# Eight segments instead of seven, nineteen sorted groups instead of sixteen, and two PSUM areas for the late read-back, in a graph-convolution kernel

## The chip, the cores and the metric

One NeuronCore of a Trainium2 chip runs the whole program; no other core takes part. Times are device microseconds of one execution. The kernel before has a median of 4145.89 us over 3 runs (4143.61 to 4146.77). The engines are named as in the profile: PE (TensorE matmul), PEld (its weight load), DVE (VectorE), ACT (ScalarE), POOL (GpSimd), SP (SyncE, which here only issues DMAs).

## What is computed

A continuous-filter convolution over 12500 nodes with 128 features and 412500 directed edges. The edges are sorted by `dst`; `src` is random. The aggregation is by `src`, and the gather by `dst`:

```python
h   = relu(layernorm(x)) @ W_in2f                      # 12500 x 128
Wij = (ssp(edge_attr @ W_f1 + b_f1) @ W_f2 + b_f2) * edge_weight[:, None]
agg = segment_sum(h[dst] * Wij, src, 12500)            # the random side
out = x + ssp(agg @ W_o1 + b_o1) @ W_o2 + b_o2         # ssp = softplus - log 2
```

So the gather reads neighbouring rows, while the sum goes to random nodes.

## The kernel before

**Chunks and groups.** Edges are taken in chunks of 512 (`CH`), four chunks to a group, 203 groups, 810 chunks with edges in them. One loop step `k` does one chunk's message and looks ahead for the later ones: hidden layer and its logarithm (PE, ACT), window matrix `at` (DVE), block matrix `inb` (DVE), rank `free`/`top` (PE, DVE), gather product `picked` (PE, ACT), `product` (DVE), transposes `turned` (PE), scaling into `o` (DVE, L925) and at last the scatter.

**Scatter.** Each message row goes to a slot in a table in HBM that belongs to the node's block of 128 nodes. For a plain chunk `message` issues four indirect DMAs from POOL, one for each 128 rows (L938). `o` has four buffers of two chunks each, and the small copy of the place column into `o` (L932) is the first write into a buffer, so it is there that DVE waits if POOL has not yet sent the chunk that was in the buffer before.

**Sorted groups.** The groups in `SORTED` (16 before) are first permuted by matmuls so that the rows of one block come together; they hold 4 x 480 edges in place of 4 x 512. Half of each such chunk goes out with one static DMA from SP, and only two indirect DMAs a chunk remain on POOL (L1067). The permuting (classes `Permute`, `Permuted`) is spread over the 18 steps ahead of the group, on DVE and PE.

**Segments and read-back.** The groups are cut into segments (`SEGS`), each with a table of its own. A table holds `T` tiles of 128 rows for each of the 98 node blocks (one more for the blocks near the segment's own nodes); `T` follows from the messages that the segment may send to a block. Nine steps after a segment's last chunk its table begins to be read back: for each unit of one to four tiles an SP load (`load`, L1317), a DVE comparison of the place column with the node numbers (`compare`, L1339), and for each tile one fp32 matmul that sums the rows into a PSUM area, three blocks side by side (`add`, L1357). The end of such three blocks is called an *end* here: DVE then adds the area to the sums in SBUF (`keep`, L1380). Only one area is there, `room_ps`, the part of the bank `count_ps` that the constant does not use, and the unit after an end goes into the next step, after that `keep`.

**What sets the read-back's pace.** A small planner at the end of the function spreads the tiles of all segments but the last over the steps, as evenly as the segment ends allow; a step takes at most three units and, before, at most one end. From its lines the numbers are

| segment: groups, sorted | T | units, tiles | tiles a step in its stretch |
|---|---|---|---|
| 55, 8 | 10 | 294, 1012 | 6.33 from step 229 |
| 37, 4 | 7 | 196, 710 | 6.33 to step 500 |
| 31, 4 | 6 | 260, 868 | 7.12 from step 501 |
| 29, 0 | 6 | 196, 612 | 7.12 to step 708 |
| 23, 0 | 5 | 196, 506 | 7.63 from step 709 |
| 14, 0 | 3 | 98, 310 | 7.63 to step 816 |
| 14, 0 | 3 | 98, 304 | read after the loop |

**After the loop.** The last segment is read with nothing beside it, four blocks (one *quad*) to a bank, banks taken in turn from the tags `acc` and `v`. For each quad `finish` runs the output layers in five stages, one stage of five different quads per turn (`stages`): `z_out` (PE, L555) with three ACT passes, `r_out` (DVE, L560), `v_out` (PE, L564), the addition to x (DVE, L568), the store.

Of the kernel before, what the change touches and what calls it, by code (L numbers as in the profile page):

```python
# [10 lines left out]
F32 = mybir.dt.float32  # L11
# [7 lines left out]
P = 128  # L19
# [1 line left out]
CH = 512  # L21
NCHUNK = TG * P // CH
QT = CH // P
SEGS = (55,37,31,29,23,14,14)
RW = P + 1
VIEWS = 16
BG = 8
# [10 lines left out]
HQ = 9  # L38
PV = 120
WIN = PV * QT  # L40
SORTED = (*range(6,51,6),*range(63,91,7),*range(97,122,7))
NPG = len(SORTED)
FIXED = 2 * P
NEAR = 2 * P
# [22 lines left out]
def gnn_kernel(  # L67
# [588 lines left out]
    with tc.tile_pool(name="edge", bufs=2) as edge, tc.tile_pool(  # L656
        name="quad", bufs=3
# [629 lines left out]
        class Collect:  # L1287


            def __init__(self, seg):  # L1290
                self.seg = seg
                self.size = QT if seg is segs[-1] else QT - 1

                self.units = []
                b = 0
                while b < NBLK:
                    T = seg.read(b)
                    n = next(n for n in (4, 3, 2, 1)
                             if n == 1 or n * T <= UT and b % self.size % n == 0
                             and b % self.size + n <= self.size  # L1300
                             and b + n <= NBLK and seg.read(b + n - 1) == T)
                    k = ceil_div(T, UT)
                    cuts = [T * i // k for i in range(k + 1)]
                    self.units += [(b, n, t0, t1 - t0) for t0, t1 in zip(cuts, cuts[1:])]
                    b += n
                self.m, self.to, self.acc, self.done = {}, {}, {}, []
                self.banks = [("acc", 1)]
# [36 lines left out]
            def add(self, u):  # L1344
                b0, nb, t0, nt = self.units[u]
                m, to = self.m.pop(u), self.to.pop(u)
                for j in range(nb * nt):
                    b, t = b0 + j // nt, t0 + j % nt
                    i = b % self.size
                    if i == 0 and t == 0 and self.size < QT:  # L1350
                        self.acc[b // self.size] = room_ps
                    elif i == 0 and t == 0:
                        tag, bufs = self.banks[b // QT % len(self.banks)]
                        self.acc[b // QT] = psum.tile([P, QT, P], F32, name="acc", tag=tag,
# [35 lines left out]

        summed = []
        owed = []

        made = {}

# [136 lines left out]
        todo = []  # L1532
# [8 lines left out]
        units[k] = [todo[0][1:]]  # L1541
        while i < len(todo):
            k += 1
            while i < len(todo) and todo[i][0] < k and len(units.get(k, ())) < 3:
                if i + 1 < len(todo):
                    units.setdefault(k, []).append(todo[i + 1][1:])
                else:
                    units.setdefault(k, [])
                i += 1
                if todo[i - 1][1].ends(todo[i - 1][2]):  # L1550
                    break

        def x_ahead(homes):
# [276 lines left out]
```

## Time and profile before

| | us |
|---|---|
| median of 3 runs | 4145.89 |
| the profiled execution, its own time | 4140.92 |
| its span, first to last instruction | 4139.20 |
| POOL busy | 3008.6 (73%), 3132 instructions |
| PE busy | 3535.6 (85%) |
| DVE busy | 3452.6 (83%) |
| ACT busy | 1549.9 (37%) |
| DMA | 845.03 MB, mean 204 GB/s |

The span is 1.7 us below the execution's own time, and that is 5.0 us below the median of the runs shown. In the page a busy PE is modelled, and POOL's busy time leaves out what its own sequencer does between two instructions; so shares of the whole span do not say alone which engine sets the pace. For that the rows must be read by stages, with what each engine waits for.

### The profile page before, as it was taken

Reading aid. Unit: us, or ns where it says so; the run is one execution under the profiler, and the core shown is the slowest. Engines: PE = TensorE matmul, PEld = TensorE weight load, DVE = VectorE, ACT = ScalarE, POOL = GpSimd, SP = SyncE. Lnnn points to the kernel's source line nnn. Section 1 sums busy time; section 2 is a strip of 40 time slices with the busy share of each in tenths; the row PEclk is TensorE's granted clock in tenths of the full one; section 3 lists DMA queues with packets and bytes.
Section 4 is the critical chain, followed back from the end, with each engine's and each line's share of the span. In section 5 each row is a group of like instructions: output and inputs, shape, how many; then the busy total and the mean of one; then the engine's idle time right before and its main releaser. Section 6 shows DMA issues by size and latency. Waiting matters only on the chain. (4 is left out here: it accounts for less than half of the span.)

```text
span 4139.2 us, 66733 instructions
## 1 busy us (share of the span) xinstructions
PE 3535.6 (85%) x18966; PEld 2206.5 (53%) x18966; DVE 3452.6 (83%) x8858; ACT 1549.9 (37%) x2365; POOL 3008.6 (73%) x3132
## 2 busy tenths in 40 slices
PE   5777777777789999988998999898998889888978
PEld 2333333333355666655565665565665556565667
DVE  7988988887689888888999988787888878888866
ACT  3444444444334334433333333333333323333313
POOL 4777777777777777777777777777777777777740
PEclk8888989888899999999999999999999999999989
DMA  6787565666577778877778776667766867666666
GB/s 162 209 267 231 157 171 160 181 196 197 161 195 217 220 228 258 242 206 201 204 240 254 215 210 183 174 181 242 202 196 203 256 204 217 194 182 193 182 188 189
DMA packets 628969, 845.03 MB, mean 204 GB/s; under 512 B 218036, under 2 KB 461868, under 8 KB 628592
## 3 DMA queue, kind: packets, MB, share of 16 engines
q1 hardware_dynamic: 528431, 634.82, 55.6%
q0 software_dynamic: 99584, 205.74, 14.8%
q8 instruction: 153, 2.51, 0.3%
q14 instruction: 225, 1.84, 0.2%
q10 hardware_dynamic: 576, 0.13, 0.0%
HBM read 426.42 MB, written 413.84 MB: 203 GB/s over the span
## 5 line engine op out<-in xcount | busy, mean ns | idle before, releaser
L938 POOL DMA_INDIRECT slots<-o,slot x2984 | 2882.1, 966 | 949.2 <-issue 707.5
L1357 PEld LDWEIGHTS count_ps<-to,m 128*128 128x128 f32 (+1 forms) x8036 | 1004.4, 199 | 660.5 <-DVE to L1339 418.0
L1357 PE MATMUL count_ps<-to,m 128*128 128x128 f32 (+1 forms) x8036 | 1114.8, 291 | 214.8 <-DVE to L1339 171.9
L907 ACT ACTIVATE hg<-picked 128x512 f32<-128x512 f32 x810 | 481.0, 594 | 2032.6 <-PE picked L901 1882.6
L895 PE MATMUL v<-r,wf 128*128 128x512 f32 x1620 | 891.9, 634 | 6.6 <-ACT r L804 4.0
L1339 DVE TENSOR_TENSOR to<-count_ps,m 128x384 f32<-128x384 f32 (+5 forms) x1396 | 716.5, 557 | 19.4 <-PE count_ps L1357 11.5
L913 DVE SCALAR_TENSOR_TENSOR product<-v,bf_t,hg 128x512 f32<-128x512 f32 x810 | 600.7, 742 | 100.4 <-PE v L895 80.8
L920 PE MATMUL turned<-ident,product 128*128 128x128 f32 x3240 | 521.9, 286 | 26.6 <-ACT hg L907 26.2
L809 DVE TENSOR_TENSOR inb<-count_ps,blk 128x392 f16<-128x392 f32 x746 | 414.4, 556 | 131.1 <-PE count_ps L1357 91.7
L925 DVE TENSOR_TENSOR o<-turned,rcut 128x512 f32<-128x512 f32 x746 | 506.4, 679 | 0.9 <-PE turned L920 0.9
L920 PEld LDWEIGHTS turned<-ident,product 128*128 128x128 f32 x3240 | 396.5, 147 | 204.8 <-issue 117.1
L804 ACT ACTIVATE r<-r,half 128x1024 f32<-128x1024 f32 x405 | 465.3, 1149 | 13.2
L803 ACT ACTIVATE r<-z,bf 128x1024 f32<-128x1024 f32 x405 | 448.7, 1108 | 0.0
L795 PE MATMUL z<-f,wf 20*128 20x512 f32 x1492 | 432.2, 655 | 0.0
L840 DVE TENSOR_REDUCE top<-free 128x4 f32<-128x392 f32 x746 | 412.6, 553 | 3.5 <-PE free L835 3.5
L901 PE MATMUL picked<-at,near 96*128 96x512 bf16 x746 | 298.5, 400 | 100.3 <-DVE o L925 82.2
L868 PE MATMUL free<-inb,rest_of 128*128 128x392 f16 x778 | 268.5, 345 | 114.1 <-DVE top L840 109.6
L895 PEld LDWEIGHTS v<-r,wf 128*128 128x128 f32 x1620 | 301.6, 200 | 109.1 <-issue 22.5
L795 PEld LDWEIGHTS z<-f,wf 20*128 20x128 f32 x1492 | 114.7, 187 | 295.8 <-issue 291.0
L887 DVE TENSOR_SCALAR at<-rel,prow 96x512 bf16<-96x512 bf16 x746 | 267.0, 358 | 0.0
L835 PE MATMUL free<-inb,after 128*128 128x392 f16 x746 | 257.7, 345 | 6.6 <-DVE used L874 4.6
L932 DVE COPY o<-place 128x8 f32<-128x8 f32 x373 | 72.3, 194 | 212.8 <-DMA slots<-o,slot 207.0
(226 smaller groups left out, 2235.9 us busy)
## 6 DMA issues: line engine op xcount, KB each, us to landing
m<-slots SPq DMA_DIRECT2D x822, 193.5 KB
m<-slots SPq DMA_DIRECT2D x336, 258.0 KB
rel<-rel_d SPq DMA_DIRECT2D x187, 384.0 KB
slots<-zero SPq DMA_DIRECT2D x100, 516.0 KB
slots<-o,slot POOLq DMA_INDIRECT x2984
f<-in_f_n SPq DMA_DIRECT2D x404, 80.0 KB
slots<-zero SPq DMA_DIRECT2D x158, 193.5 KB
slots<-zero SPq DMA_DIRECT2D x74, 258.0 KB
```

The costliest lines, as they stand in the source:

```text
L795: nc.tensor.matmul(z[:, k, :], wf1[rows, :], self.f[rows, :], start=True, stop=True)
L803: nc.scalar.activation(r, z, AF.Exp, bias=bf1, accum_out=exps[:, i:i + 1])
L804: nc.scalar.activation(r, r, AF.Ln, bias=half, scale=0.5)
L809: nc.vector.tensor_tensor(inb, count_ps[:, None, :NBLK].to_broadcast([P, QT, NBLK]), self.blk[:, c * QT:(c + 1) * QT, None].to_broadcast([ ...
L895: nc.tensor.matmul(v, wf2, r, start=True, stop=True)
L907: nc.scalar.activation(hg, ps, AF.Copy)
L913: nc.vector.scalar_tensor_tensor(m, v, bf2_t, hg, op0=ALU.add, op1=ALU.mult)
L920: nc.tensor.transpose(ps[:, i, :], m[:, i * P:(i + 1) * P], ident)
L925: nc.vector.tensor_mul(o[:, :, :P], ps, rcut.to_broadcast([P, QT, P]))
L938: put = nc.gpsimd.indirect_dma_start(out=views[j % VIEWS], out_offset=bass.IndirectOffsetOnAxis(ap=self.slot[:, j:j + 1], axis=0), in_=o[: ...
L1339: nc.vector.tensor_tensor(to[:p, a:e, :], count_ps[:p, None, :].to_broadcast([p, e - a, P]), self.m[u][:p, a:e, P:].to_broadcast([p, e - a ...
L1357: nc.tensor.matmul(self.acc[b // self.size][:, i, :], m[:p, j, :P], to[:p, j, :], start=t == 0, stop=t == self.seg.read(b) - 1)
```

## The change

Three things change.

1. `SEGS` becomes (56,36,38,29,14,14,8,8), and `SORTED` 19 groups: 6 to 54 by sixes and 62 to 125 by sevens. The sum stays 203 groups; since three more groups hold 480-edge chunks there are 811 chunks with edges. 76 chunks are sorted and 735 plain, against 64 and 746.
2. For a segment whose first group lies two or more past the last sorted group (the flag `twin`, here the segments of 29, 14, 14, 8 and 8 groups), the areas of the read-back alternate: every second one is a bank of the tag `acc`, which the sorting and the first part of the program use earlier.
3. In the planner a step may then take two ends in place of one; three units stay the limit.

```diff
-SEGS = (55,37,31,29,23,14,14)
+SEGS = (56,36,38,29,14,14,8,8)
...
-SORTED = (*range(6,51,6),*range(63,91,7),*range(97,122,7))
+SORTED = (6, 12, 18, 24, 30, 36, 42, 48, 54, 62, 69, 76, 83, 90, 97, 104, 111, 118, 125)
...
             def __init__(self, seg):
                 self.seg = seg
                 self.size = QT if seg is segs[-1] else QT - 1
+                self.twin = seg.g0 > permuted[-1] + 1
...
                 for j in range(nb * nt):
                     b, t = b0 + j // nt, t0 + j % nt
                     i = b % self.size
+                    if i == 0 and t == 0:
+                        turns.append(b)
                     if i == 0 and t == 0 and self.size < QT:
-                        self.acc[b // self.size] = room_ps
+                        if self.twin and len(turns) % 2:
+                            self.acc[b // self.size] = psum.tile([P, QT, P], F32, name="acc")
+                        else:
+                            self.acc[b // self.size] = room_ps
...
+        turns = []
...
             k += 1
+            ends = 0
             while i < len(todo) and todo[i][0] < k and len(units.get(k, ())) < 3:
...
                 i += 1
-                if todo[i - 1][1].ends(todo[i - 1][2]):
+                ends += todo[i - 1][1].ends(todo[i - 1][2])
+                if ends > todo[i - 1][1].twin:
                     break
```

The same planner with the new numbers gives:

| segment: groups, sorted | T | units, tiles | tiles a step in its stretch |
|---|---|---|---|
| 56, 9 | 10 | 294, 1012 | 5.82 from step 233 |
| 36, 5 | 7 | 196, 710 | 5.82 to step 528 |
| 38, 5 | 7 | 294, 966 | 8.28 from step 529 |
| 29, 0 | 6 | 196, 612 | 8.28 |
| 14, 0 | 3 | 98, 310 | 8.28 to step 756 |
| 14, 0 | 3 | 98, 310 | 8.57 from step 757 |
| 8, 0 | 2 | 68, 204 | 8.57 to step 817 |
| 8, 0 | 2 | 54, 206 | read after the loop |

In all 4330 tiles in 1298 units, against 4322 in 1338. The table of zeros that clears the tables ahead of their use grows from 630 to 648 DMAs.

**POOL's queue, from the third segment's last sorted groups to the end.** `slots_123` is the table of the third segment, `slots_124` and on those of the later ones; a row stands for as many indirect DMAs as its last number says. Before:

```order
L1067 DMA slots_123<-o,slot_p 82432x129 x8
L938 DMA slots_123<-o,slot 82432x129 x64
L938 DMA slots_124<-o,slot 78336x129 x464
L938 DMA slots_125<-o,slot 64768x129 x368
L938 DMA slots_126<-o,slot 39680x129 x224
L938 DMA slots_127<-o,slot 38912x129 x216
```

and now:

```order
L1067 DMA slots_123<-o,slot_p 96000x129 x8
L938 DMA slots_123<-o,slot 96000x129 x64
L938 DMA slots_124<-o,slot 78336x129 x464
L938 DMA slots_125<-o,slot 39680x129 x224
L938 DMA slots_126<-o,slot 39680x129 x224
L938 DMA slots_127<-o,slot 26112x129 x128
L938 DMA slots_128<-o,slot 26368x129 x124
```

Over the whole queue 2984 plain and 128 sorted indirect DMAs became 2940 and 152, so 3112 became 3092.

**DVE in a late step of the loop, while a table is read.** `to` is the result of a comparison, `agg` the sums, `count_ps` the old area (`room_ps` is in its bank) and `acc` the new one. Before, in the reading of the sixth segment (units of 3 tiles, one end to a step):

```order
L913 SCALAR_TENSOR_TENSOR product<-v,bf_t,hg 128x512
L840 TENSOR_REDUCE top<-free 128x4
L1380 TENSOR_TENSOR agg<-agg,count_ps 128x384
L887 TENSOR_SCALAR at<-rel,prow 96x512
L809 TENSOR_TENSOR inb<-count_ps,blk 128x392
L1339 TENSOR_TENSOR to<-count_ps,m 128x384 x3
L925 TENSOR_TENSOR o<-turned,rcut 128x4x128
```

and now, in the reading of the seventh (units of 4 and 2 tiles):

```order
L913 SCALAR_TENSOR_TENSOR product<-v,bf_t,hg 128x512
L840 TENSOR_REDUCE top<-free 128x4
L1386 TENSOR_TENSOR agg<-agg,acc 128x384
L1386 TENSOR_TENSOR agg<-agg,count_ps 128x384
L887 TENSOR_SCALAR at<-rel,prow 96x512
L809 TENSOR_TENSOR inb<-count_ps,blk 128x392
L1340 TENSOR_TENSOR to<-count_ps,m 128x256
L1340 TENSOR_TENSOR to<-count_ps,m 128x512
L1340 TENSOR_TENSOR to<-count_ps,m 128x256
L925 TENSOR_TENSOR o<-turned,rcut 128x4x128
```

A step with two ends has two additions to `agg`, one from each area; the rest of the step stands as it did.

**PE in the reading after the loop, one quad** (numbers kept: `to_...` tells which comparison a sum waits for). Before:

```order
L555 MATMUL z_out_49136<-agg_13464,wo1_64 128x512
L564 MATMUL v_out_49723<-wo2_65,r_out_49632 128x128 x4
L1357 MATMUL acc_49712<-to_49703,m_49665 128x128 x3
L1357 MATMUL acc_49712<-to_49710,m_49687 128x128 x3
L1357 MATMUL acc_49712<-to_49732,m_49694 128x128 x3
L1357 MATMUL acc_49755<-to_49739,m_49701 128x128 x3
```

and now:

```order
L555 MATMUL z_out_49938<-agg_13814,wo1_64 128x512
L564 MATMUL v_out_50358<-wo2_65,r_out_50291 128x128 x4
L1363 MATMUL acc_50346<-to_50336,m_50280 128x128 x4
L1363 MATMUL acc_50377<-to_50344,m_50303 128x128 x4
```

On DVE, with which these sums are paired, the rows before are

```order
L560 SCALAR_TENSOR_TENSOR r_out_49675<-z_out_49136,nbo1_71,r_out_49675 128x512
L568 TENSOR_TENSOR xo_29964<-xo_29964,v_out_49680 128x512
L1339 TENSOR_TENSOR to_49732<-count_ps_157,m_49694 128x384
L1339 TENSOR_TENSOR to_49739<-count_ps_157,m_49701 128x384
L1339 TENSOR_TENSOR to_49746<-count_ps_157,m_49708 128x384
```

and now

```order
L568 TENSOR_TENSOR xo_31505<-xo_31505,v_out_50296 128x512
L1340 TENSOR_TENSOR to_50336<-count_ps_156,m_50280 128x512
L1340 TENSOR_TENSOR to_50344<-count_ps_156,m_50303 128x512
L1386 TENSOR_TENSOR agg_13814<-agg_13814,acc_50315 128x512
L560 SCALAR_TENSOR_TENSOR r_out_50322<-z_out_49938,nbo1_71,r_out_50322 128x512
L568 TENSOR_TENSOR xo_31625<-xo_31625,v_out_50327 128x512
```

A quad of the plain blocks has two units of 4 tiles in place of four of 3. Before, two of its four comparisons (`to_49732`, `to_49739`) stand behind the same turn's `r_out`; now both (`to_50336`, `to_50344`) stand a turn ahead, before the `agg` and `r_out` of the turn in which PE uses them.

## The prediction

> **What bounds the kernel now.** I read the page's costliest groups first, then POOL's own waits, then the busy times by stages, then DVE's waits in the same stages, and at last the stretch after the loop. The costliest groups (line, engine, tiles, count | busy, mean ns | idle before, and what ended it):
>
> ```profile
> L938 POOL DMA_INDIRECT slots<-o,slot x2984 | 2882.1, 966 | 949.2 <-issue 707.5
> L932 DVE COPY o<-place 128x8 f32<-128x8 f32 x373 | 72.3, 194 | 212.8 <-DMA slots<-o,slot 207.0
> ```
>
> POOL looks 73% busy, but its idle time is not a wait for others. Who ended it (us in total, times, longest):
>
> ```profile
> POOL slots L938 <- issue: 707.5, 2320, 0.3
> POOL slots L938 <- DVE o L925: 60.7, 74, 28.9
> ```
>
> 2320 of its pauses are 0.3 us long and end with nothing but its own issue. Only 60.7 us were spent waiting for `o`, 28.9 us of them before the very first DMA. The stages (start and end, length, then busy us and count of each engine, granted clock, DMA share, GB/s):
>
> ```profile
> core 0: us, PE busy (x) PEld busy (x) DVE busy (x) ACT busy (x) POOL busy (x), PEclk, DMA share, GB/s
> 203.00:1053.00 850.00, 649.03 (x2631) 305.98 (x2632) 704.49 (x2056) 377.46 (x615) 647.20 (x666) 0.88 0.65 193
> 1053.00:1104.00 51.00, 32.57 (x101) 14.21 (x101) 24.72 (x58) 14.24 (x22) 38.80 (x41) 0.77 0.56 175
> 1104.00:1767.00 663.00, 606.49 (x3491) 394.90 (x3490) 581.49 (x1460) 261.27 (x397) 503.22 (x525) 0.96 0.78 225
> 1767.00:2408.00 641.00, 581.02 (x3375) 378.05 (x3375) 575.16 (x1433) 237.42 (x358) 487.29 (x505) 0.98 0.75 220
> 2408.00:2953.00 545.00, 492.69 (x2696) 321.44 (x2695) 441.00 (x1052) 184.77 (x269) 413.86 (x431) 0.96 0.70 197
> 2953.00:3419.00 466.00, 409.38 (x2324) 273.85 (x2323) 379.16 (x883) 157.47 (x230) 353.77 (x369) 0.96 0.73 214
> 3419.00:3702.00 283.00, 250.77 (x1448) 169.18 (x1447) 238.66 (x582) 96.43 (x141) 214.85 (x224) 0.95 0.69 194
> 3702.00:3955.00 253.00, 224.54 (x1342) 153.97 (x1341) 218.46 (x510) 86.16 (x126) 191.80 (x201) 0.98 0.67 186
> ```
>
> Divide length by POOL's count. From 203 us: 850/666 = 1.276 us a DMA; 1104 to 2408: 1304/1030 = 1.266; 2408 to 3955: 1547/1225 = 1.263. Whether there is much read-back or none, sorting or none, POOL sends one indirect DMA each 1.26 to 1.28 us. That is the pace of the loop: four DMAs, 5.05 us, for a plain chunk. DVE's wait at L932, the first write into a buffer of `o` that POOL has still to send, is the other side of it: it is the time that DVE and PE had to spare. It falls as the read-back grows; the same wait in three stretches, 1104 to 2408, 2408 to 3419 and 3419 to 3955 us (with the next wait of the last):
>
> ```profile
> DVE o L932 <- DMA slots<-o,slot: 16.5, 9, 5.2
> ...
> DVE o L932 <- DMA slots<-o,slot: 97.8, 47, 5.4
> ...
> DVE o L932 <- DMA slots<-o,slot: 33.3, 16, 3.2
> DVE agg L1380 <- PE count_ps L1357: 28.8, 39, 3.0
> ```
>
> By POOL's counts the stretches have 273, 200 and 106 chunks, so the spare time is 0.06, 0.49 and 0.31 us a chunk. After the loop POOL is done, and a second bound follows: the reading of the last table with the output layers.
>
> **The change part by part.** The sum is made against the span of the profiled execution, 4139.2 us; its own time is 4140.9, and the median of the runs shown 4145.9, to which the difference is then applied.
>
> *Fewer indirect DMAs.* 3112 become 3092. Twenty at 1.266 us, the rate of the stages in which the sorted groups lie, are 25.3 us off POOL's chain (25.3 to 25.5 with the other rates). The added chunk is in the count.
>
> *More sorting.* This lies on DVE and PE beside POOL, so it costs nothing as long as they have time to spare. From 7.12 to 7.63 tiles a step the spare time falls from 0.49 to 0.31, 0.35 us a tile. At 6.33 tiles it would be 0.77 without sorting; with eight sorted groups in 273 chunks it was 0.06, so one sorted group eats (0.77 - 0.06) x 273 / 8 = 24 us of it, POOL's own saving included. The new stretch from step 233 to 528 has 296 chunks, 5.82 tiles and ten sorted groups: 0.95 - 10 x 24 / 296 = 0.14 us a chunk to spare. Cost nothing; the cover is thin.
>
> *More tiles a step late.* At 8.28 tiles the spare time is 0.31 - 0.65 x 0.35 = 0.08 us, over 228 steps; at 8.57 it is -0.02, over 60 steps. POOL has work queued, up to seven or eight chunks, so a few us lost are not lost to it. Nothing on POOL's chain. SP's loads grow by a sixth, on DMA engines that are busy 0.67 to 0.73 of the time in these rows, which leaves them under 0.85 even if all of it were such loads.
>
> *Two areas, two ends to a step.* They remove no wait from POOL's chain, so I cost them at 0 by themselves. They let the 2-tile table be read with 1.4 ends a step in its 24 steps in place of one; each end is one `agg` addition:
>
> ```profile
> L1380 DVE TENSOR_TENSOR agg<-agg,count_ps 128x384 f32<-128x384 f32 x165 | 90.2, 547 | 73.9 <-PE count_ps L1357 73.5
> ```
>
> So 24 x 0.45 x 0.55 = 6 us more on DVE, out of the queue's reserve.
>
> *The hand-over.* Here that reserve counts. The last four rows of the loop (start, length, engine, line):
>
> ```profile
> 3964.15 0.68 DVE L925 TENSOR_TENSOR o<-turned,rcut 128x512 f32<-128x512 f32 x1
> 3996.70 0.96 POOL L938 DMA_INDIRECT slots<-o,slot  x1 [0.30 <-issue]
> 3995.40 0.42 DVE L1380 TENSOR_TENSOR agg<-agg,count_ps 128x256 f32<-128x256 f32 x1 [1.10 <-PE count_ps L1357]
> 4002.47 1.94 DVE L1339 TENSOR_TENSOR to<-count_ps,m 128x384 f32<-128x384 f32 x4
> ```
>
> The last `o` is ready at 3964.83, and POOL begins on it at about 3996.70 - 3 x 1.263 = 3992.9: 28 us in reserve. In that time DVE and PE finish the sixth table, in 31 us, at 3995.8. Both ends meet within 2 us, and the last table begins at 4002.47. So whatever reserve is missing at the last step comes out on the path. I take 8 us: 6 for the ends, and 2 for 56 tiles in place of 50 in the steps after the last message. From below 0 (a full queue again); from above 28 + 4, the whole reserve gone and those steps longer.
>
> *After the loop.* One quad of the steady reading, PE, ACT and DVE:
>
> ```profile
> 4080.47 1.02 PE L555 MATMUL z_out<-agg,wo 128*128 128x512 f32 x2
> 4081.33 1.05 PE L564 MATMUL v_out<-wo,r_out 128*128 128x128 f32 x8
> 4082.22 1.50 PE L1357 MATMUL acc<-to,m 128*128 128x128 f32 x12
> 4084.12 1.60 PE L1357 MATMUL acc<-to,m 128*128 128x128 f32 x12 [0.40 <-DVE to L1339]
> 4085.56 1.02 PE L555 MATMUL z_out<-agg,wo 128*128 128x512 f32 x2
> 4081.53 0.69 ACT L557 ACTIVATE r_out<-z_out,bo 128x512 f32<-128x512 f32 x1 [2.99 <-PE z_out L555]
> 4082.25 0.75 DVE L560 SCALAR_TENSOR_TENSOR r_out<-z_out,nbo,r_out 128x512 f32<-128x512 f32 x1 [1.29 <-ACT r_out L557]
> 4082.92 0.68 DVE L568 TENSOR_TENSOR xo<-xo,v_out 128x512 f32<-128x512 f32 x1
> 4083.51 1.95 DVE L1339 TENSOR_TENSOR to<-count_ps,m 128x384 f32<-128x384 f32 x4
> 4085.37 0.68 DVE L1380 TENSOR_TENSOR agg<-agg,acc 128x512 f32<-128x512 f32 x1
> ```
>
> A quad takes 5.09 us, and it is a ring: z_out 1.06, ACT 0.72, r_out 0.67, the addition 0.59, the first comparison 0.61, twelve sums 1.44, next z_out. In the changed order both comparisons of a quad stand a turn ahead, so PE should not wait in it: z_out to v_out 0.86, v_out 0.89, sixteen sums at 1.44/12 = 0.12 us 1.92, in all 3.67, and I take 3.75. DVE's own work is shorter: 0.67 + 0.59 + two wide comparisons + 0.6, some 3.1 us by these starts and this row of four wide ones:
>
> ```profile
> 4114.29 2.48 DVE L1339 TENSOR_TENSOR to<-count_ps,m 128x512 f32<-128x512 f32 x4
> 4024.27 0.68 DVE L1380 TENSOR_TENSOR agg<-agg,acc 128x512 f32<-128x512 f32 x1
> ```
>
> The fifth quad is added at 4024.27, so the first five take 21.8 us from 4002.47 and are bound by PE and landings; there I count 1 us each for four tiles less. Seventeen steady quads give 17 x 1.34 = 22.8. The last quads keep four units. Together 27 us off; from below 15 if the first five and half of the rest gain nothing, from above 31.
>
> The sum: -25.3 - 27 + 8 = -44.3 us, 4094.9 for the span, 4101.6 against the median.
>
> *A rule that speaks against it.* POOL's time for one DMA is 38.80/41 = 0.946 us where DVE is 48% busy and 191.80/201 = 0.954 where it is 86% busy. The Trainium skill, "SBUF — State Buffer", section "SBUF: two separate sides", says that DVE in certain modes holds a port pair which GpSimd needs to write DMA descriptors, and that GpSimd then stands still. By these two rows the added comparisons do not hold POOL up; by the rule the term would be up to their whole length, rival four.
>
> **The rivals.** *Two: the reserve is gone.* If the spare time falls by 0.6 us a tile rather than 0.35, it is -0.08 over 228 steps and -0.25 over 60, 33 us, more than the reserve. Then the hand-over costs 32 and POOL starves some 5 us: 4145.9 - 52.3 + 37 = 4131. For it speaks the near tie of the last stage, DVE busy 218.46 and PE 224.54 of 253 us; against it that POOL there still went at 253/201 = 1.26 us.
>
> *Three: the ring stays.* If PE still waits for a comparison behind `r_out`, a quad takes 1.06 + 0.72 + 0.67 + 0.59 + 0.61 + 0.97 = 4.6 us, and 17 x 0.85 = 14 us of the gain go: 4116. The rows of the program's order speak against it.
>
> *Four: POOL is held up by DVE.* About one tile a step more over 288 steps, at 0.61/4 us of comparison a tile, is 44 us on POOL's chain: 4146, no change.
>
> *Five, the other side: DVE and PE become the bound from step 529 on.* With the reserve gone only 20 us of the gain stand (52.3 - 32). The point is then 28 + 20 + 8 = 56 us lost over 288 steps, 0.19 us a step, a step of 5.24 us instead of 5.05. At 0.9 us a tile the spare time would be -0.28 and -0.54, 96 us: POOL starves for 68, 4145.9 - 52.3 + 32 + 68 = 4194. For it: three comparisons and up to two `agg` in a step, each waiting for PE (28.8 us of such waits in 106 chunks). Against it is what PE spends on a tile in the loop, 1114.8/4018 = 0.28 us by its group, a third of 0.9:
>
> ```profile
> L1357 PE MATMUL count_ps<-to,m 128*128 128x128 f32 (+1 forms) x8036 | 1114.8, 291 | 214.8 <-DVE to L1339 171.9
> ```
>
> **How the numbers follow.** My forecast, 0.66: 4101.6, alone 4089 to 4112. Rival two 0.14, three 0.06, four 0.05, five 0.09. A measurement of this kernel can tell about 0.2%, 8.3 us, from no change; one to three are faster by more (0.86), four is no change (0.05), five slower (0.09). The range holds the forecast, rival three and most of two: 4085 to 4131.
>
> **What would show it.** Right: 2940 and 152 DMAs at 1.26 to 1.28 us each; L932 waiting still after 2408 us, though less; the last POOL DMA some 25 us earlier; a steady quad near 3.75 us with no PE wait for `to`. Wrong: POOL waiting for `o` by tens of us in the last 1400 us (two, five); quads of 4.6 us or more (three); POOL's mean DMA above 0.966 us in the late stages (four). By the sum the last table begins at 4002.5 - 25.3 + 8 = 3985 us; were it later than 4000, the gain of the loop would be lost.

## The result

The changed kernel takes 4081.0 us (median of four, 4079.6 to 4084.5) beside 4146.3 us (4143.6 to 4147.7) of the kernel before on the same chip: a ratio of 0.9845, 95% interval 0.9827 to 0.9862, or 65 us less. The forecast was 44 us less and a range down to 4085. The sign held, and POOL's part of the sum nearly so; the term of the hand-over was wrong, and the one for the part after the loop too small.

The profiled execution has a span of 4082.8 us (its own time is 4084.5), 56.4 us less than the 4139.2 of before. The other 9 us stand in no stage of the profiles: the profiled execution of before (4140.9) was quicker than all four of its timed ones, that of the changed kernel was the slowest of its four. In places, with the prediction's terms:

| term (profiled executions) | forecast | measured |
|---|---|---|
| POOL's last DMA ends (3997.65, now 3976.13) | -25.3 | -21.5 |
| from there to the first comparison of the last table (4.82, now 4.44) | +8 | -0.4 |
| from that comparison to the end | -27 | -34.5 |
| sum | -44.3 | -56.4 |

POOL is still the bound of the loop, at the same pace. Its group on the page of the changed kernel, and then three stages of the late read-back (start and end, length, busy us and count of PE, PEld, DVE, ACT, POOL, granted clock, DMA share, GB/s):

```profile
L938 POOL DMA_INDIRECT slots<-o,slot x2940 | 2839.8, 966 | 939.8 <-issue 695.0
```

```profile
2516.00:3108.00 592.00, 526.63 (x3177) 365.33 (x3176) 501.89 (x1220) 198.88 (x290) 449.74 (x467) 0.98 0.76 217
3108.00:3670.00 562.00, 509.09 (x3105) 356.22 (x3103) 495.80 (x1151) 192.54 (x280) 426.38 (x445) 0.98 0.79 232
3670.00:3935.00 265.00, 239.19 (x1454) 169.96 (x1451) 238.77 (x552) 89.40 (x130) 201.24 (x210) 0.97 0.69 193
```

592/467, 562/445 and 265/210 are 1.27, 1.26 and 1.26 us a DMA, with 8.3 to 8.6 tiles a step now. DVE's spare time, its wait at L932 in the same three stretches:

```profile
DVE o L932 <- DMA slots<-o,slot: 16.5, 12, 3.9
...
DVE o L932 <- DMA slots<-o,slot: 33.5, 18, 3.8
...
DVE o L932 <- DMA slots<-o,slot: 7.2, 3, 3.7
```

By chunk (467/4, 445/4, 210/4) that is 0.14, 0.30 and 0.14 us. It shrank, but it did not run out. In the first two stretches the plan has the same 8.28 tiles a step; the first reads the third segment over one area, the second reads with two, and there DVE's spare time is twice as long.

The hand-over. DVE's rows and then POOL's last ones:

```profile
3940.08 0.68 DVE L925 TENSOR_TENSOR o<-turned,rcut 128x512 f32<-128x512 f32 x1
...
3965.53 0.42 DVE L1386 TENSOR_TENSOR agg<-agg,acc 128x256 f32<-128x256 f32 x1 [0.34 <-PE acc L1363]
...
3967.48 3.68 DVE L545 TENSOR_TENSOR xr<-xr,bo 128x512 f32<-128x512 f32 x6
3971.09 1.68 DVE L545 TENSOR_TENSOR xf<-xf,bo 128x512 f32<-128x512 f32 x4
3980.57 0.69 DVE L1340 TENSOR_TENSOR to<-count_ps,m 128x512 f32<-128x512 f32 x1 [7.81 <-DMA m<-slots]
```

```profile
3967.00 0.96 POOL L938 DMA_INDIRECT slots<-o,slot  x1 [0.30 <-issue]
3968.26 5.34 POOL L938 DMA_INDIRECT slots<-o,slot  x1 [0.30 <-DVE xr L545]
...
3975.17 0.96 POOL L938 DMA_INDIRECT slots<-o,slot  x1 [0.30 <-issue]
```

Two things are to be seen. From the last `o` (3940.76) to the last sum (3965.95) DVE and PE need 25.2 us for 56 tiles, where before they needed 31.0 for 50 (the tiles are the plan's; by PE's rows the sums of 60 and of 56 tiles start in these stretches). They are done 10 us ahead of POOL, and DVE then waits 7.81 us for the load of the last table. And one of POOL's last DMAs takes 5.34 us in place of 0.96. In the profile of before the longest of POOL's last twenty is 1.17 us.

What went from the reading is DVE's wait for PE's sums before it can add an area. The two longest of them in the old stretch:

```profile
3972.48 0.56 DVE L1380 TENSOR_TENSOR agg<-agg,count_ps 128x384 f32<-128x384 f32 x1 [4.64 <-PE count_ps L1357]
...
3992.68 0.55 DVE L1380 TENSOR_TENSOR agg<-agg,count_ps 128x384 f32<-128x384 f32 x1 [4.90 <-PE count_ps L1357]
```

All of them add up to 15.0 us before and 5.2 now, when the longest is 2.21.

One steady quad after the loop (PE, and DVE's wait):

```profile
4010.61 1.02 PE L555 MATMUL z_out<-agg,wo 128*128 128x512 f32 x2
4011.47 1.05 PE L564 MATMUL v_out<-wo,r_out 128*128 128x128 f32 x8
4012.36 1.95 PE L1363 MATMUL acc<-to,m 128*128 128x128 f32 x16
4012.39 0.75 DVE L560 SCALAR_TENSOR_TENSOR r_out<-z_out,nbo,r_out 128x512 f32<-128x512 f32 x1 [0.40 <-ACT r_out L557]
4014.14 1.02 PE L555 MATMUL z_out<-agg,wo 128*128 128x512 f32 x2
```

3.54 us in place of 5.09; PE waits for nothing, and DVE's wait for `r_out` is 0.40 in place of 1.29. A tile's sum is two instructions of PE in these rows, so x16 stands for 8 tiles; where a time is given for one sum below, it is that of one such instruction.

### The profile page after: what moved, and what is told of

It reads as the page before. It is cut to its first block, busy times and chain, and to the rows that moved or that the text cites. A ratio compares the mean times of both kernels' runs of the same rounds, so it can differ in the third digit from the quotient of the medians.

```text
span 4082.8 us, 67401 instructions
## 1 busy us (share of the span) xinstructions
PE 3503.8 (86%) x19157; PEld 2195.8 (54%) x19157; DVE 3510.2 (86%) x9073; ACT 1560.8 (38%) x2384; POOL 2989.1 (73%) x3112
## 5 line engine op out<-in xcount | busy, mean ns | idle before, releaser
L938 POOL DMA_INDIRECT slots<-o,slot x2940 | 2839.8, 966 | 939.8 <-issue 695.0
L907 ACT ACTIVATE hg<-picked 128x512 f32<-128x512 f32 x811 | 481.8, 594 | 1989.1 <-PE picked L901 1839.3
L1363 PEld LDWEIGHTS count_ps<-to,m 128*128 128x128 f32 (+1 forms) x6818 | 839.2, 198 | 576.7 <-DVE to L1340 374.8
L1363 PE MATMUL count_ps<-to,m 128*128 128x128 f32 (+1 forms) x6818 | 928.0, 289 | 210.2 <-DVE to L1340 166.7
L895 PE MATMUL v<-r,wf 128*128 128x512 f32 x1622 | 883.4, 628 | 4.4 <-ACT r L804 2.4
L1340 DVE TENSOR_TENSOR to<-count_ps,m 128x384 f32<-128x384 f32 (+2 forms) x1396 | 718.0, 557 | 35.2 <-DMA m<-slots 22.2
L925 DVE TENSOR_TENSOR o<-turned,rcut 128x512 f32<-128x512 f32 x735 | 498.0, 678 | 4.0 <-PE turned L920 3.7
L895 PEld LDWEIGHTS v<-r,wf 128*128 128x128 f32 x1622 | 300.5, 199 | 108.2 <-issue 20.7
L1363 PEld LDWEIGHTS acc<-to,m 128*128 128x128 f32 x1842 | 226.8, 196 | 79.9 <-issue 33.6
L1363 PE MATMUL acc<-to,m 128*128 128x128 f32 x1842 | 241.6, 282 | 24.4 <-DVE to L1340 23.7
```

The costliest lines, as they stand in the source:

```text
L895: nc.tensor.matmul(v, wf2, r, start=True, stop=True)
L907: nc.scalar.activation(hg, ps, AF.Copy)
L925: nc.vector.tensor_mul(o[:, :, :P], ps, rcut.to_broadcast([P, QT, P]))
L938: put = nc.gpsimd.indirect_dma_start(out=views[j % VIEWS], out_offset=bass.IndirectOffsetOnAxis(ap=self.slot[:, j:j + 1], axis=0), in_=o[: ...
L1340: nc.vector.tensor_tensor(to[:p, a:e, :], count_ps[:p, None, :].to_broadcast([p, e - a, P]), self.m[u][:p, a:e, P:].to_broadcast([p, e - a ...
L1363: nc.tensor.matmul(self.acc[b // self.size][:, i, :], m[:p, j, :P], to[:p, j, :], start=t == 0, stop=t == self.seg.read(b) - 1)
```

## The experiments

Open were: whether the terms add, what made the quads short (the order or fewer tiles), what made the hand-over cost nothing, and where the 5.34 us come from. The kernel before was timed beside each set, each on another chip; its medians were 4150.5, 4144.0, 4144.8 and 4142.9 us, and on a fifth chip 5446.4. Runs of different sets are compared by their ratios to it. Two more kernels, the 19 sorted groups alone on the kernel before and 21 groups on the changed one, gave no result; so the price of the 20 DMAs rests on the difference of two runs.

### The changed kernel again

> The changed kernel once more, nothing altered. In its first profile one indirect DMA of the last chunk (at 3968.26 us) took 5.34 us in place of 0.96, and POOL's last DMA ended at 3976.1. Theory A (the issue time of the indirect DMAs sets the loop, the long one was chance): it does not come back, POOL ends at 3971 to 3973, and the profiled execution's own time is about 4080. Rival B (the long DMA belongs to the changed end of the loop, where six tables' loads and the last messages meet): it comes back within the last 10 us of POOL, end at 3976. The median is 4081 by both; what the run also gives is the spread between a profiled execution and the median, which is 9 us too large to be a term of the sum.

Measured: 4091.2 us (4080.4 to 4094.7) beside 4150.5, ratio 0.9858 (0.9842 to 0.9874), 59 us less; the profiled execution 4080.4. The same kernel spreads over 14 us from one execution to the next here, which is the size of the 9 us above. The long DMA came back, 5.54 us at 3963.78, so on this point A fell and rival B held: it belongs to the changed order (what holds it, the later runs tell). POOL ended at 3971.84 all the same, not at B's 3976 but 4.3 us before its end in the first profile; that difference arose in the first 400 us.

### Old sorted groups, new segments

```diff
-SORTED = (6, 12, 18, 24, 30, 36, 42, 48, 54, 62, 69, 76, 83, 90, 97, 104, 111, 118, 125)
+SORTED = (*range(6,51,6),*range(63,91,7),*range(97,122,7))
```

> The changed kernel with the old 16 sorted groups: new segments, two areas, two ends to a step, but 3112 indirect DMAs as before. Theory A (the terms add, each in its own place): POOL ends where it did before (3997.7, within 2 us), the first comparison of the last table follows 4.4 us later, and the part after the loop is 34 us shorter: 4146 - 34.5 = 4111 us. Rival B (DVE's reserve matters, rival two of the prediction): with 24 us of sorting work per group given back there is more spare time, which changes nothing for POOL if A holds; by B POOL would end earlier than before and the time fall below 4106. Rival C (half of the whole gain came with fewer DMAs upstream): 4125 or more.

Measured: 4114.9 us (4112.8 to 4117.2) beside 4150.5, ratio 0.9913 (0.9899 to 0.9927), 36 us less; the changed kernel in the same set was 24 us below it. The terms add, as A said: the new segments with areas and ends bring the part after the loop, which is 33 us shorter than before, and the 24 us left for the 20 DMAs are near the 25.3 forecast. POOL's end is A's one miss: 4003.85 and not 3997.7. Of those 6 us the long DMA, 5.74 us here, makes 4.8.

### One block to a unit in the last table

```diff
-                    n = next(n for n in (4, 3, 2, 1)
+                    n = next(n for n in ((4, 3, 2, 1) if seg is not segs[-1] else (1,))
```

> The changed kernel with the last table read one block to a unit: four units of two tiles to a quad in place of two units of four. The number of tiles, sums and bytes of the quad is that of the changed kernel, the order of the quad is that of the kernel before (comparisons run half a quad ahead, not a whole one). Theory A (the order, the ring through r_out, made the old quad long): the steady quad is 1.06 + 0.72 + 0.67 + 0.59 + 0.45 + 1.0 = 4.5 us in place of 3.54, 17 quads x 0.95 = 16 us, the time about 4097, and PE waits for `to` in each quad. Rival B (fewer tiles alone shortened the quad): it stays at 3.5 to 3.7 us and the time at 4081 to 4084.

Measured: 4108.8 us (4108.7 to 4109.4) beside 4150.5, ratio 0.9898 (0.9882 to 0.9914). A steady quad of this kernel, PE's rows with one of DVE:

```profile
4030.53 1.02 PE L555 MATMUL z_out<-agg,wo 128*128 128x512 f32 x2
...
4032.32 0.75 DVE L560 SCALAR_TENSOR_TENSOR r_out<-z_out,nbo,r_out 128x512 f32<-128x512 f32 x1 [1.25 <-ACT r_out L557]
...
4034.05 1.16 PE L1363 MATMUL acc<-to,m 128*128 128x128 f32 x8 [0.71 <-DVE to L1340]
...
4035.05 1.02 PE L555 MATMUL z_out<-agg,wo 128*128 128x512 f32 x2
```

4.52 us, with the wait for `to` back: the sum of the ring, made before the run, was 4.5. With the same tiles, sums and bytes, the old order (in four small comparisons and loads, not two wide ones) costs 0.97 us a quad. From POOL's end to the end of the span it took 125.1 us, against 106.7 in the changed kernel: 18.4 us. The time is 17.6 us above that of the changed kernel in this set, where A had 16.

### The kernel before, compared one unit further ahead

```diff
             last.compare(1)
+            last.compare(2)
...
-                if u + 2 < len(last.units):
-                    last.compare(u + 2)
+                if u + 3 < len(last.units):
+                    last.compare(u + 3)
```

> The kernel before with the comparisons of the last table three units ahead in place of two (four units to a quad as before). Theory A (in the old quad PE waited 0.40 us for a comparison that stands behind the ring through r_out; without the wait PE's own work is the bound: 0.86 + 0.89 + 24 sums at 0.12 = 4.65 us): the steady quad falls from 5.09 to 4.6 to 4.7 us, no wait of PE for `to`, 17 x 0.42 = 7 us: 4139. Rival B (DVE or the m loads set the quad of 12 tiles): it stays at 5.09 and the time at 4146.

Measured: 4132.1 us (4126.7 to 4139.7) beside 4144.8, ratio 0.9971 (0.9962 to 0.9980), 13 us less. The quad, PE's rows:

```profile
4054.53 1.02 PE L555 MATMUL z_out<-agg,wo 128*128 128x512 f32 x2
...
4056.28 2.84 PE L1357 MATMUL acc<-to,m 128*128 128x128 f32 x24
...
4058.96 0.60 PE L555 MATMUL z_out<-agg,wo 128*128 128x512 f32 x1
```

4.43 us: without the wait PE's own work is the bound, as A said, and it is shorter than A's 4.65 since a sum takes 0.111 us when 24 stand in a row (2.84 less the tail of the last, 2.68 from start to next `z_out`) and not 0.12. So the old quad of 5.09 held 0.66 us of order and 0.89 us of tiles (4 tiles, 8 sums, fewer at 0.111), which is the whole of the 1.55 us gained. In the quad of 8 tiles the old order would cost 0.97.

### One area and one end to a step; then two areas and one end

```diff
-                self.twin = seg.g0 > permuted[-1] + 1
+                self.twin = False
```

> The changed kernel with one PSUM area and one end to a step, segments and sorted groups as changed. By the plan 1.95 units a step are then read from step 789 on in place of 2.68, and the sixth table ends ten steps later, with 104 tiles after the last message in place of 56. Theory A (the second area and the second end shorten the reading behind the last message, 0.45 us a tile in the changed kernel against 0.62 in the kernel before, where DVE stood 2 to 5 us before each sum): 104 x 0.62 = 64 us after the last message against a reserve of 26 and the wait of 8: the last table begins some 25 to 35 us later, 4081 + 30 = 4111 beside 4146, and DVE's waits for PE's sums return. Rival B (only the number of tiles counts): 104 x 0.45 = 47 us, 13 us later, 4094. Rival C (the prediction's term: nothing by itself, the sums are hidden): 4081.

Measured: 4112.1 us (4108.3 to 4115.7) beside 4144.0, ratio 0.9922 (0.9908 to 0.9935): 31 us more than the changed kernel, within 1 us of A. POOL ended at 3967.95, but the first comparison of the last table came at 4007.06. From the last `o` to the last sum it took 58.5 us, 0.56 us a tile. The second part alone:

```diff
-                if ends > todo[i - 1][1].twin:
+                if ends:
```

> The changed kernel with both PSUM areas, but one end to a step: the plan is that of the run with one area (104 tiles behind the last message, the sixth table ending ten steps later), the areas are those of the change. That run took 44 us from POOL's end to the first sum's hand-over more than the changed kernel, by 64 us of reading behind the last message, 0.62 us a tile. Theory A (the areas shorten each tile's reading): 104 x 0.45 = 47 us, of which 26 + 8 are covered: 13 us later than the changed kernel, 4081 + 13 = 4094 beside 4146. Rival B (the areas give nothing, the number of tiles alone counts): as the run with one area, 4112.

This run fell on a chip that granted a clock of 0.84 (5391.7 us beside 5446.4). POOL's wait there,

```profile
POOL slots L938 <- DVE o L925: 1070.9, 346, 28.5
```

shows another bound of the loop, so the time says nothing of the hand-over. Once more on a chip with the clock of the other runs:

> The changed kernel with both PSUM areas and one end to a step once more, on a chip that grants the usual clock. On the chip that granted 0.84, POOL waited for `o` through most of the loop, so its time said nothing of this question; the reading behind the last message took 60.5 us there, against 58.5 with one area and one end on the usual chip. Theory A (the areas shorten each tile's reading): 47 us from the last `o` to the last sum, the first comparison 13 us later than in the changed kernel, 4094 beside 4146. Theory B, the likelier now (with one end to a step a second area has nothing to hide, only the two ends to a step shorten the reading): 56 to 61 us, and 4108 to 4114 as with one area.

Measured: 4096.9 us (4093.8 to 4098.3) beside 4142.9, ratio 0.9890 (0.9873 to 0.9906). The guess that had become the likelier, B, fell: the second area does shorten each tile. The last `o` and the last sum in the two kernels, with one area:

```profile
3944.22 0.68 DVE L925 TENSOR_TENSOR o<-turned,rcut 128x512 f32<-128x512 f32 x1
...
4002.98 0.42 DVE L1386 TENSOR_TENSOR agg<-agg,count_ps 128x256 f32<-128x256 f32 x1 [0.65 <-PE count_ps L1363]
```

and with two areas, one end to a step:

```profile
3936.89 0.68 DVE L925 TENSOR_TENSOR o<-turned,rcut 128x512 f32<-128x512 f32 x1
...
3985.38 0.41 DVE L1386 TENSOR_TENSOR agg<-agg,acc 128x256 f32<-128x256 f32 x1
```

58.5 and 48.2 us for the same 104 tiles of the plan, 0.56 and 0.46 us a tile. (By PE's rows the sums of 111.5 and of 104 tiles start in these stretches, so by them it is 0.52 and 0.46, and part of the gain was made before the last `o`.) What went is DVE's wait for the sums: with one area it stands before an addition until PE has filled the only area. That wait, from 3936 us on, with one area and with two:

```profile
DVE agg L1386 <- PE count_ps L1363: 30.2, 21, 3.6
```

```profile
DVE agg L1386 <- PE count_ps L1363: 17.8, 8, 3.0
```

The second end to a step then leaves 56 tiles in place of 104 behind the last message (25.2 us). In this order the two steps are worth 13 and 19 us by the ratios (0.9922, 0.9890, 0.9845), each uncertain by some 10; beside the second run of the changed kernel (0.9858) the last is 13.

### Areas and ends alone on the kernel before

```diff
+                self.twin = seg.g0 > permuted[-1] + 1
...
-                        self.acc[b // self.size] = room_ps
+                        if self.twin and len(turns) % 2:
+                            self.acc[b // self.size] = psum.tile([P, QT, P], F32, name="acc")
+                        else:
+                            self.acc[b // self.size] = room_ps
...
-                if todo[i - 1][1].ends(todo[i - 1][2]):
+                ends += todo[i - 1][1].ends(todo[i - 1][2])
+                if ends > todo[i - 1][1].twin:
```

> The kernel before with the second PSUM area and two ends to a step for its segments behind the last sorted group, and nothing else: seven segments, 16 sorted groups, 3112 indirect DMAs. Theory A (areas shorten the reading behind the last message, and what DVE does next then falls into POOL's time): DVE ends the sixth table some 6 to 9 us earlier than 3995.8, its ten additions of `bo` begin before POOL's last DMA (3997.65 before), one of the last DMAs takes 3 to 5.5 us in place of 0.96, POOL ends up to 4 us later and the time is 0 to +4 us: 4146 to 4150. Rival B (the hand-over was bound by DVE and PE and the areas free it): the time falls by more than 4 us, below 4142.

Measured: 4145.5 us beside 4144.8, ratio 1.0003 (0.9994 to 1.0013): no change. From the last `o` (3964.94) to the last sum (3989.39) it took 24.5 us in place of 31.0, as A said, and what DVE does next slid under POOL. POOL was the later of the two before, by 2 us, so the quicker reading had nothing to bring forward; and POOL now ended at 4003.35, 5.7 us later, 4.3 of it by the long DMA in the second rows. DVE's rows, then POOL's:

```profile
3988.97 0.42 DVE L1386 TENSOR_TENSOR agg<-agg,count_ps 128x256 f32<-128x256 f32 x1 [1.10 <-PE count_ps L1363]
...
3990.92 3.68 DVE L545 TENSOR_TENSOR xr<-xr,bo 128x512 f32<-128x512 f32 x6
3994.53 1.68 DVE L545 TENSOR_TENSOR xf<-xf,bo 128x512 f32<-128x512 f32 x4
```

```profile
3991.76 5.29 POOL L938 DMA_INDIRECT slots<-o,slot  x1 [0.30 <-DVE xr L545]
```

In the profile of before no indirect DMA took over 2.1 us. The long one appears there too once DVE's additions begin before POOL is done.

### The additions' operand in PSUM; the additions later

```diff
-            nc.vector.tensor_add(xi, xi, spread(bo2[:p, :], xi.shape[1]))
+            nc.vector.tensor_add(xi, xi, spread(bias_of[0][:p, :], xi.shape[1]))
...
+            bias_of[0] = psum.tile([P, QT, P], F32, name="bias", tag="acc")[:, 0, :]
+            nc.scalar.activation(bias_of[0], bo2, AF.Copy)
             for _ in x_early:
```

> The changed kernel; the ten additions of `bo` to `xr` and `xf` behind the loop (5.4 us of DVE, at 3963 to 3968 us) stay in their place, but their second operand is read from PSUM, where ScalarE copies `bo` first. In three profiles of the changed order one of POOL's last three to five DMAs takes 5.0 to 5.7 us in place of 0.96 and ends just when these additions end; in the kernel before, the additions began at 3997.25, when POOL was done. Theory A (DVE's additions with both operands in SBUF keep POOL from its work; with one operand in PSUM they do not, as the comparisons with a PSUM operand, whose DMAs take 0.95 us): the long DMA is gone, POOL ends 4 to 5 us earlier after its first message and the time is 4 to 5 us less than the changed kernel's (4076 beside a kernel before of 4146). Rival B (what holds the DMA is the transfers of x into `xr` and `xf`, or the m loads): it stays at 5 us or more, time unchanged. Rival C (any DVE work holds it): it stays.

Measured: 4077.2 us (4076.5 to 4082.7) beside 4144.0, ratio 0.9838 (0.9825 to 0.9852). DVE's rows and POOL's last:

```profile
3971.65 3.67 DVE L547 TENSOR_TENSOR xr<-xr,bias 128x512 f32<-128x512 f32 x6
3975.24 1.67 DVE L547 TENSOR_TENSOR xf<-xf,bias 128x512 f32<-128x512 f32 x4
```

```profile
3970.95 0.96 POOL L940 DMA_INDIRECT slots<-o,slot  x1 [0.30 <-issue]
3972.21 0.96 POOL L940 DMA_INDIRECT slots<-o,slot  x1 [0.30 <-issue]
```

The additions are as long and overlap POOL's last DMA, and none is held. Only the last begins among them here, so other runs must bear on it too. In the next the additions were moved behind POOL's end:

```diff
             last.compare(1)
+            for w in biases[:2]:
+                x_bias(*w)
+            del biases[:2]
...
                     stages(q)
                     q += 1
+                    if biases:
+                        x_bias(*biases.pop(0))
```

> The changed kernel with the same ten additions moved: two behind the first two comparisons of the last table, then one to a quad, all after POOL's last DMA. Theory A (they hold POOL): the long DMA is gone and POOL ends 4 to 5 us earlier; of that DVE gives back 0.2 us a quad for eight quads, whose spare time is 0.40 us against 0.6 for an addition: 2 to 3 us less in all than the changed kernel (4078 beside 4146). Rival B (the transfers hold it): POOL ends as before, 3976, and the time is 1 to 2 us more.

Measured: 4078.6 us (4074.9 to 4083.1), ratio 0.9839 (0.9825 to 0.9852); no DMA over 1.4 us in the last 500 us, POOL's end at 3973.54. The steady quad stayed at 3.54 us, and from the first comparison to the end it took 103.1 us against 102.2, so the additions cost 0.9 us there at most. That the additions hold POOL is shown by their moves in both directions; that it is the operand in SBUF rests on the run above and on the next two, which keep it in PSUM. The gain in time, about 3 us by the ratios, is inside the intervals: neither run is established as faster than the changed kernel.

### More sorted groups

Both with the additions' operand in PSUM, 22 and 20 sorted groups:

```diff
+SORTED = (6,12,18,24,30,36,42,48,54, 62,67,73,78,84,89,95,101,106,112,117,123,128)
```

```diff
+SORTED = (6,12,18,24,30,36,42,48,54, 62,68,74,81,87,94,100,107,113,120,126)
```

> The changed kernel with the additions' operand in PSUM and 22 sorted groups, five and six groups apart from 62 to 128: 24 indirect DMAs fewer less four for one chunk more, 20 fewer, and three groups' sorting more before chunk 516. Theory A (POOL's count sets the loop while its lead over `o` lasts; 12 us of lead per sorted group, falling by 3 to 5 us a group at this density): the lead reaches 0 near chunk 470, POOL waits some 5 to 15 us, and of 20 x 1.266 = 25 us 10 to 20 remain: 4077 - 15 = 4062 beside 4144. Rival B (DVE is the bound of the sorted stage already, with 19 us of waits left in it between 1115 and 2516): three groups of 24 us of sorting against 19 + 20 us of lead cost all of the gain, 4075 to 4085.

> The changed kernel with the additions' operand in PSUM and 20 sorted groups, six and seven groups apart from 62 to 126: 8 indirect DMAs fewer. Theory A: the lead stays above 0 and POOL ends 8 x 1.266 = 10 us earlier: 4067 beside 4144. Rival B (DVE is the bound): 4075 or more, with POOL waiting for `o` by 8 us or more between 1700 and 2520 us.

Measured: 22 groups 4096.5 us (4094.6 to 4099.6) beside 4144.8, ratio 0.9883 (0.9868 to 0.9898); 20 groups 4079.0 us (4072.7 to 4084.1), ratio 0.9844 (0.9831 to 0.9858). With 22, 20 DMAs fewer made the kernel some 19 us slower than with 19 groups. Here POOL waits for `o`, in the whole run and, in the second row, between 1761 and 2516 us alone:

```profile
POOL slots L940 <- DVE o L927: 92.6, 85, 28.6
...
POOL slots L940 <- DVE o L927: 32.4, 26, 4.2
```

With 19 groups and the same additions the first row is

```profile
POOL slots L940 <- DVE o L927: 56.8, 63, 28.8
```

POOL ended at 3988.60, 15 us later than the 3973.17 with 19 groups, though it sent 20 DMAs fewer. So rival B held in that the work ahead of `o` is the bound of the sorted stage, though the time is 11 us above its 4085; whether DVE itself or PE before it is the bound, these rows do not tell. With 20 POOL ended at 3963.40, 10 us earlier, as A said (its profiled execution was 4072.7), but the median over five executions, which spread over 11 us, does not show it. No version beat the changed kernel by more than these runs can tell.

These two runs also settle what holds the long DMA. In each of them four DMAs begin among the ten additions with the operand in PSUM, and each takes 0.95 or 0.96 us. With 22 groups one more begins under a single addition that comes earlier and still reads `bo` from SBUF. DVE's rows and POOL's:

```profile
3978.26 0.68 DVE L547 TENSOR_TENSOR xr<-xr,bo 128x512 f32<-128x512 f32 x1
...
3982.23 3.68 DVE L547 TENSOR_TENSOR xr<-xr,bias 128x512 f32<-128x512 f32 x6
```

```profile
3978.41 1.36 POOL L940 DMA_INDIRECT slots<-o,slot  x1 [0.30 <-DVE to L1342]
...
3983.86 0.95 POOL L940 DMA_INDIRECT slots<-o,slot  x1 [0.30 <-DVE xr L547]
```

## Why the prediction was wrong, and where it was right

*Fewer indirect DMAs* held. 20 x 1.266 = 25.3 was forecast; POOL ended 21.5 us earlier, and with the 4.4 us taken off by which one DMA was held, 25.9. *More sorting* at 0 held as well, because three groups more were just carried: 22 groups were not. Its cover was thinner than the 0.14 us a chunk forecast: L932's waits from 1115 to 2516 us are 19.2 us in some 297 chunks, 0.06.

*More tiles a step late* was costed at 0 from a slope of 0.35 us of spare time a tile, with 0.08 and -0.02 us a chunk left. Measured are 0.14 to 0.30. But the slope itself was not far off; what it left out is the second area. In the run with one area DVE does not wait at L932 at all from 3108 to 3935 us, and before `agg` it waits much longer. Its row from 3108 to 3670, and with two areas and one end to a step the wait at L932 in the same stretch:

```profile
DVE agg L1386 <- PE count_ps L1363: 42.6, 46, 1.7
```

```profile
DVE o L932 <- DMA slots<-o,slot: 27.3, 17, 3.8
```

So over one area the spare time is gone, as near to the forecast as these waits can tell, with POOL still at its pace; the second area, costed at 0, gave it back.

The step that failed is *the hand-over*: +8 forecast, -0.4 measured. The fault in it is that two areas and two ends were costed at 0 by themselves. The forecast kept the reading behind the last message as it was in the old profile (31 us for 50 tiles, 0.62 a tile), added 2 us for six tiles more, and took 6 us off POOL's reserve of 28. Measured, the reserve fell by 2 only, to 26 (from 3940.76 to POOL's 3967.00; with one area it was 18), and the reading became shorter: with the areas and ends it is 0.45 us a tile, and 56 tiles take 25.2 us. So POOL is the later of the two by 10 us, 4.4 of them the held DMA's, and nothing of the reading comes out on the path. What the step should have looked at is DVE's wait before `agg` for the only area: 1.10 us in the prediction's own row, 15.0 in the whole stretch. On the old segments this is worth nothing (1.0003), since there POOL was already the later by 2 us; on the new ones it is worth 31 us. So a part that does nothing alone can carry the rest.

*After the loop* is a second term that was off, by size alone: -27 forecast, -34.5 measured. The mechanism, the ring through `r_out`, is shown in both directions (4.52 with the old order, 4.43 for the old tiles with a new one). Of the 7.5 us missing, the first and last quads have most. These rows are the fifth quad's `z_out` before and now, and the twentieth's:

```profile
4029.55 1.02 PE L555 MATMUL z_out<-agg,wo 128*128 128x512 f32 x2
...
4105.93 1.02 PE L555 MATMUL z_out<-agg,wo 128*128 128x512 f32 x2
```

```profile
3999.99 1.02 PE L555 MATMUL z_out<-agg,wo 128*128 128x512 f32 x2
...
4053.07 1.02 PE L555 MATMUL z_out<-agg,wo 128*128 128x512 f32 x2
```

From POOL's end to the fifth, 31.9 before and 23.9 now, 8.0 less, 0.4 of it the hand-over's, where 5 were counted; the fifteen quads between, 76.4 and 53.1, 23.3 less (forecast 22.8 for seventeen); from the twentieth to the end of the span 33.3 and 29.7, 3.5 less where nothing was counted. In the steady quads the gain was 1.55 us and not 1.34: 0.14 of the difference because a sum takes 0.111 us and not 0.12, the rest because 3.67 had been rounded up to 3.75.

Rival two (the reserve gone) and five (DVE and PE the bound from step 529) did not come: from 2516 to 3935 us POOL waited for `o` 7.0 us in all, never more than 0.3 at a time. What they describe came with 22 groups, though in the sorted stage, not in the late one. Rival three is what the run with one block to a unit does. *Rival four* is true in small, and of other work than it named: a DMA took 5.34 us against 0.96 under additions of two SBUF tiles, and none was held with the second operand in PSUM. Of the comparisons, for which the prediction asked it, nothing of the kind is seen: one of their two inputs is a tile from PSUM, and POOL's mean DMA stayed at 0.966 us. By the Trainium skill, "SBUF — State Buffer", section "Who interferes with whom", a DVE instruction with two SBUF inputs contends with a GpSimd instruction that reads SBUF, and one with at most one SBUF input, outside the 2-port modes, does not. The trace agrees if the indirect DMA counts as such a reader, which no run here tests. The same section has it from a probe that `tensor_tensor` did not stall a DMA; here it held this indirect one, and the measurement decides.

The lower end of the range, 4085, lies below the 4089.6 to which the terms' own lower ends add up (-25.3 with 0 and -31). It failed by 4 us, and 31 was no bound for a term that came out at 34.5. But the measured terms, -56.4 in all, would put the median at 4089.5, still inside; what carries it to 4081.0 is the 9 us between profiled and timed executions that stand in no stage. In its second timing the same kernel stood at a ratio of 0.9858, which is 4087 beside 4145.9. So that the number fell outside the range is in part chance, and that it would have lain inside by the second timing would have been chance as well: the sum missed 12 us in its terms, 8.4 of them at the hand-over and 7.5 after the loop, with 3.8 the other way on POOL's chain.

## What to carry to other kernels

When a program ends one stage on the later of two chains, cost both chains under the change, each with its own new pace, and ask what slides under the other once one of them is early. A wait of an engine for a single buffer is spare time that a second buffer gives back, but it shows in the time only where that engine is the later one. Engine work that is hidden is not free if it holds up the engine that sets the pace: look at the longest instances of the bound instruction, not at its mean.

## What the runs showed of the hardware

An indirect DMA of POOL that begins while DVE adds two SBUF tiles lasts until 0.83 to 0.84 us after the addition has ended, if that is later than its usual 0.96 us, and one that begins in a row of ten such additions until 0.83 or 0.84 us after the last. (Two, begun within 0.02 us of the addition's own start in the run with the old sorted groups, were not held.) DVE's addition and POOL's DMA in the profile of before:

```profile
3993.62 0.68 DVE L545 TENSOR_TENSOR xr<-xr,bo 128x512 f32<-128x512 f32 x1
```

```profile
3993.96 1.17 POOL L938 DMA_INDIRECT slots<-o,slot  x1 [0.31 <-issue]
```

The addition ends at 3994.30, the DMA at 3995.13. In the changed kernel the tenth ends at 3972.77 and the held DMA at 3973.60.

The chip of the first run with one end granted a clock of 0.84 in place of 0.95, and the kernel before and its variant both took 31 to 32% longer there. DVE's, ACT's and POOL's instructions are as long as elsewhere (0.681, 0.594 and 0.962 us for L925, L907 and L938), PE's are longer (0.683 us in place of 0.626 for L895), and POOL waits 1071 us in all for `o`. That the slower PE is the whole of it is not shown: its instructions are longer by 9%, the program by 31%. The ratio of the variant to the kernel before was the same on both chips, 0.9891 and 0.9890.
